# Linear attention with memories and experts on one core: values in tiles of their own, spare rows stored early, and local sums issued together with the memories

## The chip, the cores and the metric

The kernel runs on one core of a Trainium2 chip. The metric is the device time of one execution in microseconds (us). A core has five engines that run side by side: TensorE (PE in the profile; its weight loads are PEld), VectorE (DVE), ScalarE (ACT), GpSimd (POOL) and SyncE (SP), which issues most DMAs. Each engine works through its own instructions in the order of the program.

## The reference

All arithmetic is float32. The input is x with 4 batches of 1024 tokens and 256 channels; the attention has 16 heads of 16 channels and 4 memories, the expert part 8 experts of 176 hidden channels, two for each token, and a shared expert of 352.

```python
xn = layernorm(x)
q, k, v = split(xn @ w_q.T), split(xn @ w_k.T), split(xn @ w_v.T)
sq, sk = elu(q) + 1, elu(k) + 1
# memories: a coarse one (the sum of the four) and a weighted mean of the four
coarse = (sq @ M) / clip(sq . z);  M, z = memories.sum(0), norms.sum(0)
fine = sum_m w[m] * (sq @ memories[m]) / clip(sq . norms[m]);  w = softmax(mean over tokens)
p = sigmoid(relu(coarse @ eg_w1.T + b1) @ eg_w2.T + b2)
memory_output = p * fine + (1 - p) * coarse
# causal linear attention in chunks of 128, carrying the state S and its norm z
scores = (sq_c @ sk_c.T) * tril
local = (scores @ v_c + sq_c @ S) / clip(scores.sum(-1) + sq_c . z)
S, z = S + sk_c.T @ v_c, z + sk_c.sum(0)
attn = (gate * memory_output + (1 - gate) * local) @ w_o.T
# experts
cw = top-2 of softmax(xn @ gate_weight.T), normalised
y = sum_e cw[e] * down_e(silu(gate_e(xn)) * up_e(xn)) + shared expert of xn
out = x + attn + y
```

## The kernel before

**Tiles.** The 4096 tokens are 8 blocks of 512 (`blk`), each of 4 tiles of 128 (32 tiles, `n`). The heads' sums of values carry a column of ones, so a head has 17 columns in a `va` tile.

**Order.** The whole program is written out in order by Python code. Small functions each issue one unit of work. A unit is a tuple of a weight, a function and its arguments. `mix` merges several streams of units: each unit gets the rank (weight done before it + half its own) / (weight of its stream), and the streams are merged by rank. Nothing reorders the instructions afterwards. A tile pool with `bufs=k` for a tag has k buffers; a new tile of the tag waits until an old one is free of its last reader.

**The part ahead.** A string of words, `ahead`, lists the order in which blocks are prepared: `S4a` and `S4b` are `statistics` of the halves of block 4 (the mean and variance of two tiles each on VectorE; after the second, `rstd` is made by a VectorE add at L330 and a GpSimd power at L331), `N4` is `normalize` (a `shift` on VectorE at L338, two tiles normalized by VectorE at L345 and two by ScalarE at L350, the DMA of the block into `xns` in DRAM at L354, and two of the waiting loads of `loads`), `T4` is `transpose_x`, which transposes on TensorE and copies by ScalarE to `xnT`, and `V4a`, `V4b` are `values`, which multiply two tiles each by `wvg` on TensorE (L384). ScalarE copies the result to `va` (L389) and the router's logits to `lgs` (L393), and GpSimd writes ones and zeros (L394, L395). `va` lies in the same tile as the block's x (`wide`, tag `tok` of the pool `big`, 8 buffers): the values overwrite the normalized rows. Other words of the string are `masks`, `memories`, `living`, `route`, `exps` and `gates`.

**After it.** SP issues eight DMAs that copy x into `sums` in DRAM (L1250), then two that store zeros to the spare rows of `sums` and of `xns` (L1251, L1252). The zeros lie in the tile `zero`, of the tag `wide` with 3 buffers, which `count_i`, the exponentials of `project` (L627, L628) and `shared_gate` use as well. Then a first merge runs the first projections (`project` on TensorE, `projected` on VectorE) beside the steps of `sorting`, which rank the tokens by expert. `batch_weights` and `odd_keys` end it.

**Rounds.** `attention_round(n)` is the list of units of tile n: `scores` (TensorE, into the PSUM tile `quad`, of which there is one; it also needs the odd heads' keys `skO` from ScalarE, L700), four `mask` (VectorE reads `quad`, L720), `turned(n - 2)`, `keys_back`, `output(n - 2)` for n - 2 below `held_from` = 24, `memory` (TensorE, over `quad`, L828), `weigh` (VectorE, L838 to L843), `gate_hidden(n - 1)` (L903 to L909), `fine` in two halves (VectorE reads `quad`, L857), `local` (TensorE, L739, and a ScalarE copy, L746), `gate_out(n - 1)` (L915 to L918), `back` (L755 to L779), `update` and `odd_keys(n + 1)`. In rounds 0 and 1 the units of `lists` are merged in: for each batch of three tiles, `invert` makes one-hots on VectorE (L562, L566), `hold` scales them on ScalarE and GpSimd (L579, L582), and `add_slots` adds them up in the PSUM tile `found` (L590). In rounds 2 to 29 the experts are merged in: `expert_turn` (L1061 to L1067), `expert_hidden` (L1074 to L1081), `expert_out` (L1087, L1091) and `put`, a scatter that adds into `sums` (L1096). `level`, `cap` and `share` decide how much of the experts' work each round gets, by the weights of its units. Rounds 30 and 31 and what is left of the outputs follow, with additions of the expert sums on GpSimd (`total`) and the stores. Small PSUM results share a pool of 4 banks (`bank`).

Of the kernel before, what the change touches and what calls it, by code (L numbers as in the profile page):

```python
# [22 lines left out]
def linear_attention_moe_kernel(  # L23
# [62 lines left out]
    big = ctx.enter_context(tc.tile_pool(name="big", bufs=NBLK))  # L86
# [13 lines left out]
    def load_x(blk):  # L100

        wide = big.tile([P, NT, VW], FP, tag="tok", name=f"x_{blk}")
        xb = wide[:, :, :H]
        parts = 2 if blk == 0 else 1
        n = NT // parts
        for part in range(parts):
            rows = slice((blk * NT + part * n) * P, (blk * NT + (part + 1) * n) * P)
            (nc.scalar if part else nc.sync).dma_start(
                xb[:, part * n : (part + 1) * n],
                x[rows, :].rearrange("(n p) h -> p n h", p=P),  # L110
            )
        st["x", blk] = xb
        st["wide", blk] = wide
# [25 lines left out]
    wk = load_weight(w_k, "wk")  # L139
    b2 = const.tile([P, 1], FP, tag="b2", name="b2")  # L140
# [174 lines left out]
    def statistics(blk, half):  # L315

        xb = st["x", blk]
        if half == 0:
            st["norm", blk] = (
                small.tile([P, NT, 2], FP, tag="mv", name=f"mv_{blk}", bufs=3),  # L320
                small.tile([P, NT], FP, tag="rstd", name=f"rstd_{blk}", bufs=3),
            )
        mv, rstd = st["norm", blk]
        n = NT // 2
        for i in range(half * n, (half + 1) * n):
            stats = small.tile([P, 6], FP, tag="stats", name=f"stats_{blk}_{i}")
            nc.vector.bn_stats(stats, xb[:, i, :])
            nc.vector.bn_aggr(mv[:, i, :], stats)
        if half:
            nc.vector.tensor_scalar(rstd, mv[:, :, 1], LN_EPS, None, ALU.add)  # L330
            nc.gpsimd.tensor_tensor(rstd, rstd, neghalf, ALU.pow)  # L331

    def normalize(blk):

        xb = st["x", blk]
        mv, rstd = st.pop(("norm", blk))
        shift = small.tile([P, NT], FP, tag="shift", name=f"shift_{blk}")
        nc.vector.scalar_tensor_tensor(  # L338
            shift, mv[:, :, 0], -1.0, rstd, ALU.mult, ALU.mult
        )  # L340
        xnT = io.tile([P, NC, TB], FP, tag="xnT", name=f"xnT_{blk}")
        st["xnT", blk] = xnT
        half = NT // 2
        for i in range(half, NT):
            nc.vector.tensor_scalar(  # L345
                xb[:, i, :], xb[:, i, :], mv[:, i, 0:1], rstd[:, i : i + 1],
                ALU.subtract, ALU.mult,
            )
        for i in range(half):
            nc.scalar.activation(  # L350
                xb[:, i, :], xb[:, i, :], AF.Identity,
                bias=shift[:, i : i + 1], scale=rstd[:, i : i + 1],
            )
        nc.sync.dma_start(  # L354
            xns[blk * TB : (blk + 1) * TB, :].rearrange("(n p) h -> p n h", p=P), xb
        )
        for _ in range(2):
            if loads:
                loads.pop(0)()
# [14 lines left out]
    def values(blk, pair):  # L374

        xnT, wide = st["xnT", blk], st["wide", blk]
        if pair == 0:
            st["va", blk] = wide[:, :, : NH * D1].rearrange("p i (h k) -> p i h k", k=D1)
        va = st["va", blk]
# [14 lines left out]
        nc.gpsimd.memset(va[:, tiles, :, HD:D1], 1.0)  # L394
        nc.gpsimd.memset(wide[:, tiles, NH * D1 :], 0.0)  # L395
# [154 lines left out]
    def invert(lo):  # L550
# [3 lines left out]
        if lo == 0:  # L554
            st["found"] = bank("found")
# [31 lines left out]
    def add_slots(lo):  # L587
        places, held = st.pop(("held", lo))
        for k in range(min(3, 2 * NTT - lo)):
# [231 lines left out]
    def memory(n):  # L821
# [3 lines left out]
        for c in range(NC):  # L825
            for g in range(NG):
# [4 lines left out]
                )  # L831

# [343 lines left out]
    def attention_round(n):  # L1176
# [10 lines left out]
        u += unit(1280, output, n - 2, False) if n - 2 < held_from else []  # L1187
        u += unit(560, memory, n) + unit(64, weigh, n)

        u += unit(256, gate_hidden, n - 1) + unit(64, fine, n, 0)  # L1190
        u += unit(560, local, n) + unit(64, fine, n, 1)
# [30 lines left out]
    ahead = "S0a S0b S1a N0 T0 S1b S2a N1 V0a T1 V0b S2b S3a N2 V1a T2 V1b masks S3b S4a N3 V2a T3 V2b"  # L1222
    ahead += " memories S4b S5a N4 V3a T4 V3b living S5b S6a N5 V4a T5 V4b route exps S6b S7a N6 V5a T6"
    ahead += " V5b S7b N7 V6a T7 V6b gates V7a V7b"
# [4 lines left out]
    with tc.tile_pool(name="ps_v", bufs=2, space=bass.MemoryType.PSUM) as ps_v:  # L1229
        for what in ahead.split():  # L1230
# [3 lines left out]
            blk, half = int(what[1]), "ab".find(what[2:])  # L1234
            if what[0] == "S":
                statistics(blk, half)
            elif what[0] == "N":
                normalize(blk)
            elif what[0] == "T":
                for pair in range(NT // 2):  # L1240
# [10 lines left out]
    nc.sync.dma_start(sums[T:, :], zero[:, :H])  # L1251
    nc.sync.dma_start(xns[T:, :], zero[:, :H])  # L1252


    def sorting():
# [4 lines left out]
        yield from owners()  # L1260

    first_pairs = queries(0) + queries(1) + keys(0) + shared(0) + keys(1) + queries(2)
# [15 lines left out]
    batches = list(range(0, 2 * NTT, 3))  # L1278
    for k, lo in enumerate(batches):
        lists += [(400, invert, lo)]  # L1280
        lists += [(100, hold, batches[k - 1])] if k else []
        lists += [(768, add_slots, batches[k - 2])] if k > 1 else []
# [10 lines left out]
    def weight(units):  # L1293
        return sum(u[0] for u in units)
# [86 lines left out]
```

## Time and profile before

| | us |
|---|---|
| median of 3 runs | 717.58 |
| lowest and highest run | 713.74, 719.43 |
| the profiled execution's own time | 711.61 |
| its span, first to last instruction | 709.9 |
| TensorE busy | 653.3 |
| VectorE busy | 451.6 |
| GpSimd busy | 387.9 |
| ScalarE busy | 267.0 |

The mean granted clock of TensorE is 0.979. The part ahead ends about 54 us into the span, the first projections and the sort about 93, rounds 0 and 1 about 146, and round 29 about 660. A wait is put down to the instruction whose end released the waiting one.

### The profile page before, as it was taken

Reading aid. Unit: us, or ns where it says so; the run is one execution under the profiler, and the core shown is the slowest. Engines: PE = TensorE matmul, PEld = TensorE weight load, DVE = VectorE, ACT = ScalarE, POOL = GpSimd, SP = SyncE. Lnnn points to the kernel's source line nnn. Section 1 sums busy time; section 2 is a strip of 40 time slices with the busy share of each in tenths; the row PEclk is TensorE's granted clock in tenths of the full one; section 3 lists DMA queues with packets and bytes.
Section 4 is the critical chain, followed back from the end, with each engine's and each line's share of the span. In section 5 each row is a group of like instructions: output and inputs, shape, how many; then the busy total and the mean of one; then the engine's idle time right before and its main releaser. Section 6 shows DMA issues by size and latency. Waiting matters only on the chain.

```text
span 709.9 us, 14253 instructions
## 1 busy us (share of the span) xinstructions
PE 653.3 (92%) x5084; PEld 465.9 (66%) x5084; DVE 451.6 (64%) x1196; ACT 267.0 (38%) x614; POOL 387.9 (55%) x439
## 2 busy tenths in 40 slices
PE   4897979989999989999999999999898998898986
PEld 3773456667777766676676666677676775566665
DVE  5654878856666667665756756655767665556653
ACT  2663354424444344334333343344334433323310
POOL 3310036446776745565655645657767576556556
PEclk9999999999999999999999999999999999999999
DMA  9556000045556643343453443455555474553474
GB/s 301 181 184 193 0 1 1 24 125 141 133 137 135 137 90 92 85 100 90 92 110 81 103 92 80 98 123 126 105 136 117 112 169 88 129 118 65 96 236 166
DMA packets 86483, 81.52 MB, mean 115 GB/s; under 512 B 7549, under 2 KB 84013, under 8 KB 86285
## 3 DMA queue, kind: packets, MB, share of 16 engines
q1 hardware_dynamic: 71085, 60.40, 29.3%
q0 software_dynamic: 13632, 18.62, 15.8%
q10 hardware_dynamic: 1696, 1.58, 0.7%
q8 instruction: 41, 0.67, 0.4%
q14 instruction: 29, 0.24, 0.1%
HBM read 62.62 MB, written 22.15 MB: 119 GB/s over the span
## 4 chain that ended last, share of the span: by engine, by line
PE 78%; DVE 10%; DMA 4%; ACT 4%; issue 2%; POOL 1%; SPq 1%; DVEq 0%; ACTq 0%; POOLq 0%
PE phe L1074 12%; PE pye L1087 9%; PE po L980 6%; PE psu L943 6%; PE pg L929 5%; PE quad L713 5%; PE pk L622 4%; PE pn L739 4%; PE po L984 4%; PE quad L828 4%; PE pq L622 3%; PE pte L1061 2%; PE found L590 2%; PE pv L384 2%; PE pte L1065 2%
## 5 line engine op out<-in xcount | busy, mean ns | idle before, releaser
L1096 POOL DMA_INDIRECT sums<-y,islot x71 | 113.4, 1597 | 71.2 <-DMA sums<-y,islot 33.7
L1074 PE MATMUL phe<-wgu,turned 128*128 128x352 f32 x276 | 97.6, 476 | 3.7 <-issue 2.3
L1080 DVE SCALAR_TENSOR_TENSOR hidden<-hidden,phe 128x176 f32<-128x176 f32 x71 | 23.8, 335 | 109.3 <-ACT hidden L1079 109.2
L720 DVE TENSOR_TENSOR sT<-quad,causal 128x512 f32<-128x512 f32 x128 | 80.5, 681 | 4.3 <-PE quad L713 3.9
L1028 POOL DMA_INDIRECT xg<-xns,islot x71 | 71.0, 1000 | 18.3 <-issue 9.8
L1087 PE MATMUL pye<-wdn,turned 88*128 88x256 f32 x284 | 76.4, 391 | 2.5 <-issue 2.4
L850 POOL TENSOR_TENSOR cg<-coarse,gates 128x256 f32<-128x256 f32 x32 | 24.5, 766 | 94.7 <-DVE h L907 59.8
L1074 PEld LDWEIGHTS phe<-wgu,turned 128*128 128x128 f32 x276 | 48.5, 192 | 26.8 <-issue 8.2
L1087 PEld LDWEIGHTS pye<-wdn,turned 88*128 88x128 f32 x284 | 49.6, 189 | 17.0 <-issue 10.9
L1091 ACT ACTIVATE y<-pye,wslot 128x256 f32<-128x256 f32 x71 | 33.6, 473 | 70.4 <-PE pye L1087 70.3
L868 POOL TENSOR_TENSOR fm<-fm 128x512 f32<-128x512 f32 x32 | 43.0, 1343 | 26.4 <-DVE fm L857 14.9
L1067 ACT COPY turned<-pte 128x512 f32<-128x512 f32 (+1 forms) x71 | 41.1, 578 | 35.1 <-PE pte L1065 33.1
L1079 ACT ACTIVATE hidden<-phe 128x176 f32<-128x176 f32 x71 | 22.6, 318 | 79.4 <-PE phe L1074 77.2
L980 PE MATMUL po<-wd,h 128*128 128x256 f32 (+1 forms) x192 | 48.3, 388 | 0.1
L929 PE MATMUL pg<-xnT,wg 128*128 128x512 f32 (+1 forms) x96 | 47.7, 621 | 0.1
L943 PE MATMUL psu<-xnT,wu 128*128 128x512 f32 (+1 forms) x96 | 46.2, 603 | 0.0
L582 POOL TENSOR_TENSOR held<-ones,two 128x213 f32<-128x213 f32 (+1 forms) x22 | 15.6, 716 | 53.1 <-DVE ones L562 53.1
L857 DVE TENSOR_TENSOR fm<-quad,rw 128x512 f32<-128x512 f32 x64 | 42.0, 679 | 0.0
L980 PEld LDWEIGHTS po<-wd,h 128*128 128x128 f32 (+1 forms) x192 | 35.6, 194 | 6.9 <-issue 0.6
L828 PE MATMUL quad<-mem,sqT 32*128 32x170 f32 x512 | 28.2, 335 | 10.3 <-DVE sT L720 10.3
L838 DVE TENSOR_SCALAR rw<-quad 128x80 f32<-128x80 f32 x32 | 7.6, 238 | 45.0 <-PE quad L828 45.0
L918 DVE SCALAR_TENSOR_TENSOR o<-diff,prob,loc 128x256 f32<-128x256 f32 x32 | 33.3, 1042 | 3.6
(210 smaller groups left out, 1403.3 us busy)
## 6 DMA issues: line engine op xcount, KB each, us to landing
wgu<-in_w_gate_dram SPq DMA_DIRECT2D x71, 176.0 KB
wgu<-in_w_up_dram SPq DMA_DIRECT2D x71, 176.0 KB
wdn<-in_w_down_dram SPq DMA_DIRECT2D x71, 176.0 KB
xns<-x SPq DMA_DIRECT2D x8, 512.0 KB
sums<-in_x_dram SPq DMA_DIRECT2D x8, 512.0 KB
x<-in_x_dram SPq DMA_DIRECT2D x7, 512.0 KB
part<-sums SPq DMA_DIRECT2D x12, 256.0 KB
out_dram<-acc SPq DMA_DIRECT2D x12, 256.0 KB
```

The source lines that it names most:

```text
L622: nc.tensor.matmul(pq, w[:, k, c * P : (c + 1) * P], xnT[:, k, :], start=(k == 0), stop=(k == NC - 1),)
L720: nc.vector.tensor_mul(sT, quad[:, g, :].rearrange("p (c t) -> p c t", t=P), causal[:, None, :].to_broadcast([P, NC * 2, P]),)
L828: nc.tensor.matmul(quad[:, g, c * KM : (c + 1) * KM], sqT[rows, c, tok], mem[rows, c, :], start=True, stop=True,)
L857: nc.vector.tensor_mul(fm[:, c].rearrange("p g m (r k) -> p g (m r) k", k=HD), quad[:, :, c * KM + KX + KN : (c + 1) * KM].rearrange("p g ...
L868: nc.gpsimd.tensor_add(fm[:, :, 0:2, :], fm[:, :, 0:2, :], fm[:, :, 2:4, :])
L929: nc.tensor.matmul(pg[:n, :], wg[:, k, f * P : f * P + n], xnT[:, k, :], start=(k == 0), stop=(k == NC - 1),)
L943: nc.tensor.matmul(pu[:n, :], wu[:, k, f * P : f * P + n], xnT[:, k, :], start=(k == 0), stop=(k == NC - 1),)
L980: nc.tensor.matmul(po[:, :H], st["h", blk, f][:k, tok], wd[:k, f, :], start=(f == 0), stop=False)
L1028: nc.gpsimd.indirect_dma_start(out=xg, out_offset=None, in_=xns, in_offset=bass.IndirectOffsetOnAxis(ap=islot[:, j : j + 1], axis=0),)
L1074: nc.tensor.matmul(ph[:, : 2 * F], xgT[:, k, :], wgu[:, k].rearrange("p g f -> p (g f)"), start=(k == 0), stop=(k == NC - 1),)
L1087: nc.tensor.matmul(py[:, :H], hT[:FH, f, :], wdn[:, f, :], start=(f == 0), stop=(f == 1))
L1096: nc.gpsimd.indirect_dma_start(out=sums, out_offset=bass.IndirectOffsetOnAxis(ap=islot[:, j : j + 1], axis=0), in_=st.pop(("y", j)), in_of ...
```

## The change

It has four parts.

1. `big` has 9 buffers. `values` takes a tile of its own for each block (`va_b`) and no longer writes over x; GpSimd fills the ones and zeros of a whole block at once, at its first half.
2. The two stores of zeros move from behind the copies of x into the list `loads`, behind `wk`. `normalize` takes two of the loads for even and three for odd blocks.
3. The string `ahead` has another order: `N` stands in front of the next block's first half of statistics, and block 0 is taken in halves all the way. `normalize` gives tiles to ScalarE and VectorE by turns. The first two batches of the lists (`invert` of two and `hold` of one) move from rounds 0 and 1 to the last steps of `sorting`; the PSUM bank of `found` is taken at the first `add_slots`.
4. `memory` and `local` become one unit of weight 1120. Where a round has no `output` left, an empty unit of 1280 takes its place in the merge. `weight`, which feeds `level` and `cap`, does not count empty units.

```diff
-    big = ctx.enter_context(tc.tile_pool(name="big", bufs=NBLK))
+    big = ctx.enter_context(tc.tile_pool(name="big", bufs=NBLK + 1))
...
-        wide = big.tile([P, NT, VW], FP, tag="tok", name=f"x_{blk}")
-        xb = wide[:, :, :H]
+        xb = big.tile([P, NT, VW], FP, tag="tok", name=f"x_{blk}")[:, :, :H]
...
     wk = load_weight(w_k, "wk")
+    loads.append(lambda: nc.sync.dma_start(sums[T:, :], zero[:, :H]))
+    loads.append(lambda: nc.sync.dma_start(xns[T:, :], zero[:, :H]))
...
-        if half:
-            nc.vector.tensor_scalar(rstd, mv[:, :, 1], LN_EPS, None, ALU.add)
-            nc.gpsimd.tensor_tensor(rstd, rstd, neghalf, ALU.pow)
+        if half or blk == 0:
+            some = slice(half * n, (half + 1) * n) if blk == 0 else slice(0, NT)
+            nc.vector.tensor_scalar(rstd[:, some], mv[:, some, 1], LN_EPS, None, ALU.add)
+            nc.gpsimd.tensor_tensor(rstd[:, some], rstd[:, some], neghalf[:, some], ALU.pow)
...
-        for i in range(half, NT):
-            nc.vector.tensor_scalar(
...
-        for i in range(half):
-            nc.scalar.activation(
...
+        for i in range(some.start, some.stop):
+            if i % 2:
+                nc.vector.tensor_scalar(
...
+            else:
+                nc.scalar.activation(
...
+        if half == 0:
+            return
...
-        for _ in range(2):
+        for _ in range(2 + blk % 2):
...
         if pair == 0:
+            wide = big.tile([P, NT, VW], FP, tag="tok", name=f"va_{blk}")
+            st["wide", blk] = wide
+            nc.gpsimd.memset(wide[:, :, NH * D1 :], 0.0)
             st["va", blk] = wide[:, :, : NH * D1].rearrange("p i (h k) -> p i h k", k=D1)
+            nc.gpsimd.memset(st["va", blk][:, :, :, HD:D1], 1.0)
...
-        nc.gpsimd.memset(va[:, tiles, :, HD:D1], 1.0)
-        nc.gpsimd.memset(wide[:, tiles, NH * D1 :], 0.0)
...
+    def memory_and_local(n):
+
+        memory(n)
+        local(n)
...
-        u += unit(1280, output, n - 2, False) if n - 2 < held_from else []
-        u += unit(560, memory, n) + unit(64, weigh, n)
+        u += unit(1280, output, n - 2, False) if n - 2 < held_from else [(1280, lambda: None)]
+        u += unit(1120, memory_and_local, n) + unit(64, weigh, n)
...
-        u += unit(560, local, n) + unit(64, fine, n, 1)
+        u += unit(64, fine, n, 1)
...
-    ahead = "S0a S0b S1a N0 T0 S1b S2a N1 V0a T1 V0b S2b S3a N2 V1a T2 V1b masks S3b S4a N3 V2a T3 V2b"
-    ahead += " memories S4b S5a N4 V3a T4 V3b living S5b S6a N5 V4a T5 V4b route exps S6b S7a N6 V5a T6"
-    ahead += " V5b S7b N7 V6a T7 V6b gates V7a V7b"
+    ahead = "S0a S0b N0a T0a N0b T0b S1a S1b N1 S2a V0a T1 V0b S2b N2 S3a V1a T2 V1b masks S3b N3 S4a"
+    ahead += " V2a T3 V2b memories S4b N4 S5a V3a T4 V3b living S5b N5 S6a V4a T5 V4b route exps S6b N6"
+    ahead += " S7a V5a T6 V5b S7b N7 V6a T7 V6b gates V7a V7b"
...
-    nc.sync.dma_start(sums[T:, :], zero[:, :H])
-    nc.sync.dma_start(xns[T:, :], zero[:, :H])
...
         yield from owners()
+        invert(batches[0])
+        yield
+        hold(batches[0])
+        invert(batches[1])
+        yield
...
-    for k, lo in enumerate(batches):
-        lists += [(400, invert, lo)]
-        lists += [(100, hold, batches[k - 1])] if k else []
-        lists += [(768, add_slots, batches[k - 2])] if k > 1 else []
+    for k, lo in enumerate(batches[2:]):
+        lists += [(400, invert, lo), (100, hold, batches[k + 1]), (768, add_slots, batches[k])]
...
     def weight(units):
-        return sum(u[0] for u in units)
+        return sum(u[0] for u in units if len(u) > 2)
```

## The prediction

> **What bounds the kernel.** First the page's busy rows and the chain by engine: TensorE sets the time, but not all of it.
>
> ```profile
> PE 653.3 (92%) x5084; PEld 465.9 (66%) x5084; DVE 451.6 (64%) x1196; ACT 267.0 (38%) x614; POOL 387.9 (55%) x439
> PE 78%; DVE 10%; DMA 4%; ACT 4%; issue 2%; POOL 1%; SPq 1%; DVEq 0%; ACTq 0%; POOLq 0%
> ```
>
> The edits leave TensorE's instructions as they are, so a gain can only come from its 57 us of idle time (709.9 - 653.3) and from stretches at a lower granted clock. I looked for both with the waits of two windows (columns: total us, times, longest us), the chain, and the busy time by stretch. The waits of 0 to 110 us:
>
> ```profile
> DVE sqT L636 <- ACT eq L628: 9.2, 3, 7.2
> ACT eq L627 <- DMA xns<-zero: 7.0, 1, 7.0
> PE pk L622 <- DVE sqT L636: 3.9, 1, 3.9
> PE found L590 <- ACT held L579: 3.6, 1, 3.6
> ```
>
> ScalarE's third exponential needs a buffer of tag `wide` that `zero` still holds; VectorE waits for that exponential, TensorE for VectorE. The chain shows why `zero` is held: its last store is queued behind eight copies of x into `sums`.
>
> ```profile
> 48.96 6.13 DMA sums<-in_x_dram
> 55.11 10.66 DMA xns<-zero
> 65.84 0.61 ACT eq L627
> ```
>
> The stretches (start:end, length, busy of PE, PEld, DVE, ACT, POOL, clock, DMA share, GB/s) show what such a gap costs afterwards:
>
> ```profile
> 65.00:70.00 5.00, 2.11 (x4) 0.86 (x5) 2.68 (x9) 3.46 (x6) 0.00 (x0) 0.86 0.02 8
> 70.00:75.00 5.00, 5.00 (x11) 2.27 (x10) 4.79 (x14) 1.82 (x3) 0.00 (x0) 0.80 0.02 5
> 95.00:100.00 5.00, 5.00 (x45) 3.94 (x45) 4.03 (x9) 2.34 (x9) 2.74 (x4) 0.66 0.01 3
> 605.00:610.00 5.00, 3.61 (x22) 2.19 (x23) 1.68 (x5) 0.65 (x2) 2.59 (x2) 0.79 0.69 161
> ```
>
> At 0.66 of full clock 1.7 us of the five are lost (0.34 x 5). A dense slow spell therefore costs about 1.7 us beyond its gap.
>
> In the middle TensorE is nearly full (98.48 us busy of 100 from 350 on). Only late rounds stand out; from 575 to 655, first the waits of PE, then the timeline of round 26 (start, duration, instruction, in brackets the idle time before it and what ended it):
>
> ```profile
> PE quad L828 <- DVE sT L720: 7.9, 4, 2.4
> 586.08 0.34 DVE L1080 SCALAR_TENSOR_TENSOR hidden<-hidden,phe 128x176 f32<-128x176 f32 x1 [2.82 <-ACT hidden L1079]
> 586.70 1.28 DVE L720 TENSOR_TENSOR sT<-quad,causal 128x512 f32<-128x512 f32 x2
> 588.04 0.86 PE L828 MATMUL quad<-mem,sqT 32*128 32x170 f32 x16 [2.04 <-DVE sT L720]
> ```
>
> `memory` overwrites `quad`, so it waits for all four masks, and the last two masks stand in VectorE's order behind an expert's `hidden`, which waits for TensorE and ScalarE. Rounds 26 to 29 have no `output` between the masks and `memory`.
>
> **The change, part by part.**
>
> *Values apart (`va_b`, a ninth `tok` buffer) and the new order ahead.* Today `va_0` overwrites x_0 and waits for the store of x_0 (4.8 us on ScalarE at 17.57; GpSimd's `rstd` of block 2 queues behind it). `va_0` takes the free buffer, and `va_b` needs only the store of x_(b-1): that wait goes. But normalize now stands ahead of the next block's first statistics:
>
> ```profile
> 34.00 0.17 DVE L330 TENSOR_SCALAR rstd<-mv 128x4 f32<-128x4 f32 x1
> 34.08 0.42 DVE L327 BATCH_NORM_STATS2 stats<-x 128x6 f32<-128x256 f32 x1
> 34.32 1.01 POOL L331 TENSOR_TENSOR rstd<-rstd,neghalf 128x4 f32<-128x4 f32 x1 [5.20 <-DVE rstd L330]
> 35.36 0.16 DVE L338 SCALAR_TENSOR_TENSOR shift<-mv,rstd 128x4 f32<-128x4 f32 x1
> ```
>
> The 1.36 us from 34.00 to 35.36 are covered by two statistics (1.16) today and will be bare. A block then costs VectorE 2.3 (statistics) + 1.36 + 0.85 (shift, two tiles) = 4.5 us, where TensorE needs 4.4 (transposes 0.87, values 3.56); masks, memories, route and gates add 7.7 us of VectorE. Walking the order: N1 ends at 13.1, N4 at 28.7, N5 at 35.3, N7 at 47.3-47.9; then T7 and three halves of values, 0.9 + 5.4, give 53.7. Today V7b ends at 54.16. The bare wait eats what the freed buffer gives. I take 0, from -1.5 to +1.5. Halving block 0 and alternating the two engines by tile only move the first transposes about 1 us ahead.
>
> *Spare rows stored early.* The two 128 KB stores now enter SP's queue behind N1 and N2 (issue 0.51 and 0.34 us, ahead of later weight loads needed only after 53 us and of later xns stores with a slack of some us). `zero` is free long before 59 us. The third exponential then starts near 59.3 instead of 65.84. TensorE saves its 3.9 us of idle and the slow spell, 1.7: -5.6. Next is VectorE, whose first late result moves by 6.3 us (67.14 to 60.8), so it does not hold TensorE. If the buffer stayed late, all 5.6 would return. Take -5.6 (bounds -6.5, -3.5). The copies into `sums` go on from 48 to 66; the first scatter into them comes after 150.
>
> *First two lists ahead of time.* Today `found` waits behind the chain of `batch_weights` on VectorE (90.7 to 93.2), then a one-hot (0.92) and ScalarE's 0.84. With two one-hots and one `hold` in the sort's steps, TensorE can run `add_slots(0)` and the next gate projection at once and next misses only the odd keys (ScalarE, behind the exponential of 91.49): scores at 92.2. What is done today by 97.08 is done at 93.3: -3.8, and about 1 us of the spell at 95-99: -4.5 (taken a little short). The added VectorE work in the sort is 2 x 0.92 us; from 85 to 90 VectorE is busy only 2.43 of 5, so it fits; uncovered it costs 1.8. Bounds -6, -2.
>
> *`local` behind `memory`, and the empty unit of 1280.* No instruction is added. The empty unit counts in the ranks of the merge, not in a round's weight; the other empty unit (3000 of the experts) stops counting too, which lowers the level from 11824 to 11724 and leaves the number of experts in every round as it is. From the weights in the listing the ranks follow: in rounds 26 to 29 no `hidden` stands between the masks any more, and between the last mask and `memory` stand 4.4, 4.4, 2.7 and 4.4 us of TensorE work (an expert product 1.2, a shared projection 1.72, `expert_out` 0.86, a turn 0.65), where nothing stood. That covers the four waits, 7.9 us. What is late next is `quad`'s return: `memory` to the next scores shrinks from about 10 to 7 us of TensorE work, and VectorE's chain (weigh 2.3, h 0.5, fine 1.3, an interposed `hidden`) takes 5.2 to 7.4. I keep 1 us for that.
>
> In rounds 2 to 25 masks already end 2.4 to 7.4 us before `memory`. In some, `hidden` now stands ahead of `weigh` (9, 11, 12, 13, 22 to 25): VectorE starts about 2.6 us later there, against a measured slack of 2.1 to 4.9 before the next scores. Conversely rounds 2, 8 and 21 lose a 2.4 us wait of `weigh`. Taken +0.6 (bounds -3, +4); uncovered, each us late is paid by TensorE.
>
> *The rule that speaks against part of this.* Two of the gaps (605 and 630) are followed by slow spells, together 3.4 us. The Trainium skill, page "TensorE: Matmul & The Clock Gate", section "Why this matters for your kernels", puts the fall at idle gaps of over about 3 us. By it, closing gaps of 1.7 us returns no clock, and this edit gives 7.9 - 1 = 6.9. The row 605:610 shows 0.79 right after a single gap of 1.74 us; by it the edit gives 7.9 + 3.4 - 1 = 10.3. Measurement decides; as a new gap may bring one such spell back, I take -9.5 (bounds -12, -4).
>
> *The tail.* Round 31's `memory` waits 2.47 us for masks at 683.02, and its spell costs 1.7; `output` 25 now covers the wait. But the ranks also put `turned(30)` ahead of output 27, and `gate_hidden(31)` with `turned(31)` behind 29 and ahead of 30. The first meets o(30) about 1.8 us early; the second bares h 0.76, prob 0.29 + 0.14, o 0.62 and the hand-overs, 2.2 us. -4.2 + 4.0: 0 (bounds -2.5, +2.5).
>
> **Sum:** 0 - 5.6 - 4.5 - 9.5 + 0.6 + 0 = -19.0. The profiled execution took 711.61 (span 709.9 and 1.7 around it), so it would take 692.6. The runs' median is 717.58, 6 us above that execution; the same -19 gives **698.6**.
>
> **Rivals.**
>
> *Only the beginning gains (0.17).* The late rounds hand `quad` back late instead, and gaps of 1.7 us return at the scores. For it: one buffer, and `memory` now 3 to 4 us later. Against: covers of 6.4 to 8.4 us. Then 0 - 5.6 - 4.5 + 0 = -10: 707.5.
>
> *More than forecast (0.12).* The other two spells of the rounds (skO 2.31 us at 544, the wait of `pye` 2.40 at 504) also vanish, as back and turn shift: -19 - 8 = 690.6. Nothing in the edits aims at them.
>
> *The stores do not free the buffer (0.05).* Another reader of that slot keeps it: -19 + 5.6, 704.2. Against: the wait names `zero`'s store alone.
>
> *Slower: `weigh` behind `hidden` (0.06).* Were it late in all 28 rounds, VectorE's 2.6 us against slacks of 1.0 to 1.4 us (rounds 4, 6, 8 and 14) would bare 1.2 us a round: 34 us, and six more spells, 10. 698.6 + 44 = 743. It decides once the mean loss passes 19 / 28 = 0.68 us a round. Against: only about eight rounds have that order, most with slack above 2.6.
>
> **Numbers.** The forecast has 0.60, its own range 692 to 705 (parts' bounds seldom all on one side). The wider range takes in the rivals at 690.6, 704 and 707.5 and a run's scatter of about 3 us (713.74 to 719.43 now): 689 to 711. About 1%, 7 us, is what this kernel's measurement can tell from no change. Faster by more: 0.58 of the forecast's 0.60, 0.14 + 0.12 + 0.04 of the rivals: 0.88; within: 0.06; slower: 0.06.
>
> **What would show it.** Right: no wait of ScalarE for `zero`, no slow stretch near 70 and 97; the first gather of xg near 136 instead of 146; no wait of L828 for sT from 565 to 640; the values ending within 1.5 us of 54; two new gaps of about 2 us ahead of L882 in the tail. Wrong: waits of L713 for `fm` at round boundaries, slow stretches in the middle beyond the two at 505 and 546, VectorE waiting in `rstd` until the values end past 56.

## The result, and the profile after

The changed kernel takes **711.65 us** (median of 20 runs, 710.04 to 716.87) against 717.14 for the kernel before on the same chip: a ratio of 0.9936, with a 95% interval of 0.9915 to 0.9958. That is 5.5 us less, where 19 had been forecast. The profiled execution of after has a span of 709.3 us and stands near its median. The one of before (711.61, span 709.9) was 5.5 us quicker than its median, so the two traces show a difference of 0.6 us where the medians show 5.5. Every set of runs below has its own runs of the kernel before (medians of 712.5 to 717.1), so ratios are compared across sets, not times.

The page of after, its busy row and the chain by engine:

```profile
PE 648.7 (91%) x5084; PEld 466.2 (66%) x5084; DVE 453.2 (64%) x1198; ACT 267.0 (38%) x614; POOL 386.4 (54%) x424
PE 69%; DVE 20%; issue 4%; ACT 3%; POOL 2%; DMA 1%; DVEq 0%; POOLq 0%; ACTq 0%
```

TensorE is busy for nearly as long as before (4.6 us less). But the chain that ended last now runs through VectorE for 20% of the span, where it was 10%.

The places that the prediction aimed at did change. The waits of 0 to 110 us in after (columns: total us, times, longest us), the rows on which the first part turns:

```profile
DVE sqT L646 <- ACT eq L638: 3.3, 4, 1.9
DVE shift L346 <- POOL rstd L334: 8.8, 8, 1.2
```

and of before, for the second of them:

```profile
DVE shift L338 <- POOL rstd L331: 5.4, 2, 4.3
```

No engine waits for the store of `zero` any more: VectorE's wait for the exponential is 3.3 us in place of 9.2, and the wait of `pk` for it is gone. The wait for `rstd` is now bare at every block, eight times for 8.8 us, where before had two for 5.4. The stretches of after that answer to the slow ones of before (start:end, length, busy of PE, PEld, DVE, ACT, POOL, clock, DMA share, GB/s):

```profile
65.00:70.00 5.00, 5.00 (x13) 2.10 (x12) 4.69 (x16) 3.05 (x5) 0.00 (x0) 1.00 0.02 5
70.00:75.00 5.00, 5.00 (x13) 2.17 (x12) 4.83 (x14) 1.01 (x2) 0.00 (x0) 1.00 0.00 0
95.00:100.00 5.00, 4.70 (x63) 3.38 (x63) 4.46 (x10) 2.71 (x9) 2.56 (x4) 1.00 0.01 3
605.00:610.00 5.00, 4.12 (x52) 3.31 (x50) 3.75 (x8) 1.46 (x3) 4.69 (x6) 1.00 0.33 87
```

The gap at 65 and the slow clocks of 0.80, 0.66 and 0.79 are gone; in the clock records of after no slow spell (a stretch at half clock) begins between 552.8 and 709.8. Round 26 in after's timeline: the last masks, the `hidden` that stood ahead of them, `memory`:

```profile
591.42 1.88 DVE L730 TENSOR_TENSOR sT<-quad,causal 128x512 f32<-128x512 f32 x3
595.77 0.34 DVE L1095 SCALAR_TENSOR_TENSOR hidden<-hidden,phe 128x176 f32<-128x176 f32 x1 [2.48 <-ACT hidden L1094]
598.33 0.86 PE L838 MATMUL quad<-mem,sqT 32*128 32x170 f32 x16
```

The masks end at 593.3, 5.0 us ahead of `memory`; that `hidden` now follows them. So what took the gain back lies elsewhere. Set the stretch from the scores of round 9 to those of round 26 ("scores 9 to 26" from here on) side by side, first before, then after:

```profile
267.00:580.00 313.00, 303.88 (x2526) 218.25 (x2525) 201.48 (x509) 117.96 (x257) 188.47 (x183) 0.99 0.46 106
```
```profile
263.00:589.00 326.00, 306.91 (x2522) 222.33 (x2522) 199.92 (x508) 117.29 (x257) 184.59 (x181) 0.97 0.45 101
```

The same work (2522 and 2526 recorded matmuls) takes 13 us longer. TensorE's idle time, length less busy, grows from 9.1 to 19.1 us, its busy time by 3.0, and the clock falls from 0.99 to 0.97. In the clock records, two slow spells became five. The sum over the whole span, in us, between the same events in both traces:

| from, to | before | after | difference | forecast |
|---|---|---|---|---|
| start, end of `values` | 54.16 | 55.60 | +1.4 | 0 |
| end of `values`, first `pr` (stores early) | 34.4 | 29.0 | -5.4 | -5.6 |
| `pr`, scores of round 0 (lists ahead) | 6.8 | 3.0 | -3.8 | -4.5 |
| scores 0, scores 3 | 66.3 | 69.2 | +2.9 | in the +0.6 |
| scores 3, scores 26 | 418.7 | 432.2 | **+13.5** | +0.6 |
| scores 26, scores 30 | 81.5 | 74.2 | -7.3 | -9.5 |
| scores 30, last `po` | 42.5 | 42.9 | +0.4 | 0 |
| last `po`, end | 5.5 | 3.2 | -2.3 | not named |

Together -0.6, between these two executions: one row has eaten what the others brought.

### The profile page after: what moved, and what is told of

It is laid out like the page before. It is cut to its first block, busy times and chain, and to the rows that moved or that the text cites. A ratio compares the mean times of both kernels' runs of the same rounds, so it can differ in the third digit from the quotient of the medians.

```text
span 709.3 us, 14219 instructions
## 1 busy us (share of the span) xinstructions
PE 648.7 (91%) x5084; PEld 466.2 (66%) x5084; DVE 453.2 (64%) x1198; ACT 267.0 (38%) x614; POOL 386.4 (54%) x424
## 4 chain that ended last, share of the span: by engine, by line
PE 69%; DVE 20%; issue 4%; ACT 3%; POOL 2%; DMA 1%; DVEq 0%; POOLq 0%; ACTq 0%
PE phe L1089 11%; PE pye L1102 8%; PE po L995 5%; PE pn L749 4%; PE psu L958 4%; PE quad L723 4%; PE pg L944 4%; PE quad L838 4%; PE po L999 4%; PE pk L632 3%; PE pq L632 3%; PE pte L1076 3%; DVE o L933 3%; PE pt L897 2%; DVE fm L872 2%
## 5 line engine op out<-in xcount | busy, mean ns | idle before, releaser
L1043 POOL DMA_INDIRECT xg<-xns,islot x71 | 70.8, 997 | 19.1 <-issue 10.3
L1089 PEld LDWEIGHTS phe<-wgu,turned 128*128 128x128 f32 x276 | 49.8, 197 | 27.8 <-issue 8.6
L933 DVE SCALAR_TENSOR_TENSOR o<-diff,prob,loc 128x256 f32<-128x256 f32 x32 | 45.3, 1416 | 3.9 <-issue 0.5
L1094 ACT ACTIVATE hidden<-phe 128x176 f32<-128x176 f32 x71 | 22.5, 317 | 63.1 <-PE phe L1089 53.4
L944 PE MATMUL pg<-xnT,wg 128*128 128x512 f32 (+1 forms) x96 | 45.4, 596 | 0.1
L756 ACT COPY nT<-pn 128x512 f32<-128x512 f32 x32 | 18.7, 585 | 47.6 <-PE pn L749 41.8
L749 PE MATMUL pn<-sT,va 128*32 128x128 f32 x1024 | 34.8, 276 | 0.0
```

The lines of the kernel that those rows point to most:

```text
L749: nc.tensor.matmul(pn[CW * r : CW * (r + 1), q, :], wide[:, i, first : first + CW], st["sT", h // 2][:, c * 2 + h % 2, :], start=True, sto ...
L933: nc.vector.scalar_tensor_tensor(o, st.pop(("diff", n)), prob, st.pop(("base", n)), ALU.mult, ALU.add)
L944: nc.tensor.matmul(pg[:n, :], wg[:, k, f * P : f * P + n], xnT[:, k, :], start=(k == 0), stop=(k == NC - 1),)
L1043: nc.gpsimd.indirect_dma_start(out=xg, out_offset=None, in_=xns, in_offset=bass.IndirectOffsetOnAxis(ap=islot[:, j : j + 1], axis=0),)
L1089: nc.tensor.matmul(ph[:, : 2 * F], xgT[:, k, :], wgu[:, k].rearrange("p g f -> p (g f)"), start=(k == 0), stop=(k == NC - 1),)
```

## The experiments

The question is which part of the change holds back rounds 3 to 25: the merged unit, the empty unit, or the order ahead; and once that is known, by what mechanism. In the diffs the lines with a minus are after's, in one case before's.

### One part undone at a time

`local` back in its own unit between the two halves of `fine`, the empty units kept:

```
-u += unit(1120, memory_and_local, n) + unit(64, weigh, n)
+u += unit(560, memory, n) + unit(64, weigh, n)
...
-u += unit(64, fine, n, 1)
+u += unit(560, local, n) + unit(64, fine, n, 1)
```

> The changed kernel with memory and local as two units again, weigh behind memory and local between the halves of fine; the empty units of 1280 stay. Theory A (the merged unit sends weigh behind an expert's hidden on VectorE and brings back's bank back late, which costs TensorE about 13 us from round 12 to 27): about 700 us, 10 to 13 below the changed kernel, weigh again within 0.3 us of memory's end in rounds 9, 11, 12, 13 and 22 to 25. Rival B (the loss of the middle is scatter between executions and local's place does not matter): 710 to 713.

Measured: 698.23 us, ratio 0.9743 (0.9706 to 0.978). The stretch from scores 9 to scores 26 is 312.5 us again, and the late rounds keep their gain (scores 26 to 30 in 73.4). So the loss came with the merged unit; whether by ranks, by VectorE's queue or by the place of `local` is asked below.

The empty unit of 1280 taken out instead:

```
-u += unit(1280, output, n - 2, False) if n - 2 < held_from else [(1280, lambda: None)]
+u += unit(1280, output, n - 2, False) if n - 2 < held_from else []
```

> The changed kernel without the empty unit of 1280 (rounds 26 to 31 then have nothing in the place of output). Theory A (the empty unit is what removed the four waits of memory for the masks, and it is worth 7 to 10 us): about 719, with waits of memory for sT of about 8 us from round 26 to 29. Rival B (the merged unit moves memory far enough by itself, and the empty unit adds only the two gaps in the tail): 709 to 712.

Measured: 712.17 us, 0.9939 (0.9916 to 0.9961), the same as after. The waits of TensorE from 575 to 655 still have nearly nothing of the masks:

```profile
PE quad L838 <- DVE sT L730: 0.9, 1, 0.9
```

So with the merged unit the empty one has little left to do: without it, scores 26 to 30 take 76.5 us in place of 74.2, and what follows 1.2 us less. A unit is ranked at the middle of its weight, so `memory` in a unit of 1120 is merged 280 later anyway, behind more of the experts' work, and `weigh` 560 later. That was the rival's reading.

The order ahead as in before (only the string `ahead`, cut here to its first part):

```
-ahead = "S0a S0b N0a T0a N0b T0b S1a S1b N1 S2a V0a T1 V0b S2b N2 S3a V1a T2 V1b masks ...
+ahead = "S0a S0b S1a N0 T0 S1b S2a N1 V0a T1 V0b S2b S3a N2 V1a T2 V1b masks ...
```

> The changed kernel with the old order of the part ahead (statistics of the next block ahead of normalize, block 0 whole); values keep their own tiles. Theory A (the bare wait for rstd cost 1.4 us or more, and it ate what the freed buffer gives): 2 to 4 us less than the changed kernel, the values ending near 52. Rival B (the part ahead is set by TensorE and by the slow spell near 37, not by VectorE's order): within 1 us of the changed kernel, the values ending at 55 to 56.

Measured: 708.49 us, 0.9896 (0.9855 to 0.9936); `values` end at 51.58 in place of 55.60. The interval overlaps that of after (0.9915 to 0.9958).

Before (the lines with a minus are before's), with nothing changed but the two stores and the number of loads that a block takes:

```
+loads.append(lambda: nc.sync.dma_start(sums[T:, :], zero[:, :H]))
+loads.append(lambda: nc.sync.dma_start(xns[T:, :], zero[:, :H]))
...
-for _ in range(2):
+for _ in range(2 + blk % 2):
...
-nc.sync.dma_start(sums[T:, :], zero[:, :H])
-nc.sync.dma_start(xns[T:, :], zero[:, :H])
```

> The kernel before with one edit: the two stores of zeros in the list of loads behind wk, and two or three loads a block. Theory A (the stall at 59 to 68 is worth 5.6 us and nothing downstream takes it back): 711.5, a ratio of 0.992. Rival B (VectorE, saturated until 85, or a later wait takes most of it): 714 to 717, a ratio over 0.995.

Measured: 712.25 us, 0.993 (0.9899 to 0.9961). From the end of `values` to the first `pr` its trace takes 28.5 us (54.10 to 82.63) against 34.4: -5.9, the size forecast.

The first and third of these together:

```
-u += unit(1120, memory_and_local, n) + unit(64, weigh, n)
+u += unit(560, memory, n) + unit(64, weigh, n)
...
-u += unit(64, fine, n, 1)
+u += unit(560, local, n) + unit(64, fine, n, 1)
...
-ahead = "S0a S0b N0a T0a N0b T0b S1a S1b N1 ...
+ahead = "S0a S0b S1a N0 T0 S1b S2a N1 ...
```

> The changed kernel with the old order ahead and with memory and local as two units again (values apart, stores, lists and empty units stay). If the two losses add: 698.2 - 3.2 = 695. If they overlap[...]: 697 to 699.

Measured: 688.18 us, **0.9632** (0.9595 to 0.9669). The sum expected, 695 where before took 716.5, is a ratio of 0.970; this is about 5 us better.

### Where the merged unit costs: ranks, VectorE's queue, or the place of `local`

Three edits of after. In the first, `memory` has 560 again, `weigh` follows it, and `local` follows `weigh`, all ahead of `fine`:

```
-u += unit(1120, memory_and_local, n) + unit(64, weigh, n)
+u += unit(560, memory, n) + unit(64, weigh, n) + unit(560, local, n)
```

> The changed kernel with the merged unit split: memory 560, weigh 64, local 560 directly behind, then gate_hidden and both halves of fine. Memory and weigh have their ranks of before; local still stands ahead of gate_hidden and of fine. Theory A (the rank of memory and weigh: weigh comes behind an expert's hidden): about 699, as with local back. Rival B (the place of local: TensorE does it early and then reaches back and the next bank before VectorE has caught up): 708 to 712.

Measured: 704.28 us (697.01 to 712.27, widely spread), 0.9834 (0.979 to 0.9879): between, as neither theory had it. `weigh` is in time here: in its trace it starts 0.07 us after `memory` in rounds 9, 11 to 13 and 22 to 25. But `gate_hidden` and the first `fine` now rank 560 later, and that seems to cost here too. It is not the whole answer: a kernel further below (`weigh` inside the merged unit) has these two equally late and is quick; it differs from this one only in the places of `memory` and `local`. What holds this kernel back stays open.

In the second, `local` stays behind `memory` but both count 560, and an empty counted unit of 560 stands where `local` was, so that every rank is the old one:

```
-u += unit(1120, memory_and_local, n) + unit(64, weigh, n)
+u += unit(560, memory_and_local, n) + unit(64, weigh, n)
...
-u += unit(64, fine, n, 1)
+u += unit(560, lambda m: None, n) + unit(64, fine, n, 1)
```

> The changed kernel with the merged unit at weight 560 and an empty unit of 560 (counted in the level) where local was, between the halves of fine. All other units have the ranks that they have with local back; only local is issued with memory. Theory A (ranks): 698 to 700. Rival B (the place of local in TensorE's order): 708 to 712. Between: both.

Measured: 693.51 us, 0.971 (0.9668 to 0.9751), as good as `local` put back, within the intervals. Where TensorE does `local` does not show in the time; the ranks of the others do.

In the third, `gate_out` is put ahead of the second half of `fine`, which keeps VectorE's `o` away from GpSimd's half of `fm`:

```
-u += unit(64, fine, n, 1)
-u += unit(64, gate_out, n - 1) + unit(528, back, n) + unit(300, update, n)
+u += unit(64, gate_out, n - 1) + unit(64, fine, n, 1)
+u += unit(528, back, n) + unit(300, update, n)
```

> The changed kernel with gate_out ahead of the second half of fine, so that o no longer runs beside GpSimd's sums of fm. Theory C (o, 1416 ns a time instead of 1042 with GpSimd beside it, lengthens the chain to back's loc and so the hold on the bank, about 0.4 to 1 us in many rounds): o falls to about 0.5 us and the time by 4 to 8 us, to 704 to 708. Rival A (the chain is late because weigh starts late; o's length is a small part): within 2 us of 711.7.

Measured: 709.83 us, 0.9925 (0.9884 to 0.9966): no gain over after that stands clear of the scatter. The groups of instructions, after and then this kernel (count | busy us, mean ns | idle before):

```profile
L933 DVE SCALAR_TENSOR_TENSOR o<-diff,prob,loc 128x256 f32<-128x256 f32 x32 | 45.3, 1416 | 3.9 <-issue 0.5
```
```profile
L933 DVE SCALAR_TENSOR_TENSOR o<-diff,prob,loc 128x256 f32<-128x256 f32 x32 | 16.4, 514 | 3.6
```

`o` fell from 1416 to 514 ns, 29 us of VectorE in all, and the median hardly moved. A slow `o` is not what cost the 13 us. It may be worth a part: at a mean clock of 0.983 to 0.985 this kernel took 703.4 to 703.8 us, where after at 0.983 took 710.2 to 712.4, and scores 9 to 26 take 319.5 us in its trace in place of 326.2, with `weigh` as late as in after. About 2 us of that may be the set of runs: at 0.979, before took 711.0 to 712.3 in this one and 713.4 to 714.8 in the one with `local` back. At 0.966 to 0.974 the kernel took 711.1 to 714.2, so slow spells decide more about its median than `o` does.

### `weigh` itself

If the late rank of `weigh` is the cause, a kernel with `memory` at its old rank and `weigh` 560 later must be slow, and one that brings only `weigh` forward must be quick. In the first of the two, `gate_hidden` and the first `fine` stand behind `weigh` and are 560 later with it; the second is the cleaner test.

```
-u += unit(1120, memory_and_local, n) + unit(64, weigh, n)
+u += unit(560, memory_and_local, n) + unit(560, lambda m: None, n) + unit(64, weigh, n)
```

> The changed kernel with memory and local merged at weight 560 and then an empty unit of 560 (counted in the level), so that memory and local stand where they did with the merged unit of 560, and weigh and fine are as late as in the changed kernel. Theory A1 (the late rank of weigh on VectorE is the cause): ratio 0.988 to 0.996, like the changed kernel. Theory A2 (the late rank of memory on TensorE): 0.968 to 0.975, as with the merged unit at 560.

Measured: 722.79 us, 1.0089 (1.0059 to 1.0119): slower than before, and far from the quick kernels. It is worse than the range that I had put down. From scores 9 to 26 it takes 327.3 us, as after does (326.2); the rest is lost earlier, where scores 0 to 9 take 184.3 us against 175.3. Rounds 0, 2, 3 and 8 account for it (9.3 us; the others win 0.3 back). In rounds 2 and 8 `weigh` starts 4.45 and 3.40 us after `memory` here, and 0.40 and 0.22 in after.

The opposite, `weigh` put into the merged unit, with its weight added (so that `memory` itself ranks 32 later), and the order ahead of after:

```
+def memory_local_weigh(n):
+    memory_and_local(n)
+    weigh(n)
...
-u += unit(1120, memory_and_local, n) + unit(64, weigh, n)
+u += unit(1184, memory_local_weigh, n)
```

> The changed kernel with weigh inside the merged unit: memory and local are as late as in the changed kernel, but weigh stands directly behind them on VectorE, ahead of an expert's hidden of the same stretch. Theory A1 (weigh behind hidden): ratio 0.970 to 0.978. Theory A2 (memory's late rank): 0.988 to 0.996. With both, between the two.

Measured: 691.29 us, **0.9626** (0.9575 to 0.9677), better than the range expected. Against before, this is a larger gain than the one forecast for the change, and it is after with one unit changed. Scores 9 to 26, 310.4 us:

```profile
260.00:570.00 310.00, 298.52 (x2522) 216.92 (x2522) 196.25 (x506) 117.17 (x257) 186.63 (x183) 0.99 0.46 107
```

TensorE is idle for 11.5 us in place of 19.1 and busy 8.4 us less, at a clock of 0.99. There is one slow spell where after has five; at the prediction's 1.7 us each, the four make about 6.8 of the 8.4 (an estimate). How many spells a run has varies: the mean clock of this kernel's runs lies between 0.978 and 0.995.

What VectorE waits for in that stretch tells the mechanism. First before, then after, then this kernel:

```profile
DVE hidden L1080 <- ACT hidden L1079: 51.3, 23, 5.4
DVE rw L838 <- PE quad L828: 38.5, 11, 4.9
```
```profile
DVE hidden L1095 <- ACT hidden L1094: 80.8, 23, 7.7
DVE rw L853 <- PE quad L838: 4.2, 2, 2.7
```
```profile
DVE rw L858 <- PE quad L838: 40.6, 12, 4.9
DVE hidden L1100 <- ACT hidden L1099: 38.0, 21, 4.9
```

`rw` is the first instruction of `weigh`. In before, VectorE comes to it early and waits there for `memory`, 38.5 us in all. In after it hardly waits there: it stands at an expert's `hidden`, with `weigh` queued behind, while `quad` is long ready. Without that, the 40 us of waiting are back at `rw`, where VectorE waits for TensorE and not TensorE for VectorE. The late-`weigh` kernel shows after's picture (83.6 at `hidden`, 4.2 at `rw`), the one with all ranks of 560 shows before's (53.5 and 37.5).

Round 22 shows a single case. After's timeline (start, duration, instruction, idle time before it and its releaser), with `memory`, the expert's `hidden`, `weigh`, `o`, `loc` and TensorE's next `pye`:

```profile
517.96 0.86 PE L838 MATMUL quad<-mem,sqT 32*128 32x170 f32 x16
521.60 0.34 DVE L1095 SCALAR_TENSOR_TENSOR hidden<-hidden,phe 128x176 f32<-128x176 f32 x1 [7.05 <-ACT hidden L1094]
522.22 0.23 DVE L853 TENSOR_SCALAR rw<-quad 128x80 f32<-128x80 f32 x1
526.35 1.89 DVE L933 SCALAR_TENSOR_TENSOR o<-diff,prob,loc 128x256 f32<-128x256 f32 x1
528.89 0.42 DVE L783 TENSOR_TENSOR loc<-pb,rden 128x256 f32<-128x256 f32 x1
529.37 1.13 PE L1102 MATMUL pye<-wdn,turned 88*128 88x256 f32 x4 [0.99 <-DVE loc L783]
```

The same round with `weigh` in the unit:

```profile
507.92 0.86 PE L838 MATMUL quad<-mem,sqT 32*128 32x170 f32 x16
509.15 0.24 DVE L858 TENSOR_SCALAR rw<-quad 128x80 f32<-128x80 f32 x1 [4.64 <-PE quad L838]
511.56 0.34 DVE L1100 SCALAR_TENSOR_TENSOR hidden<-hidden,phe 128x176 f32<-128x176 f32 x1 [0.61 <-ACT hidden L1099]
516.15 0.42 DVE L783 TENSOR_TENSOR loc<-pb,rden 128x256 f32<-128x256 f32 x1
517.11 1.13 PE L1107 MATMUL pye<-wdn,turned 88*128 88x256 f32 x4
```

`memory` ends at 518.82 in after, yet `rw` starts at 522.22, 3.40 us later, behind a `hidden` for which VectorE had waited 7.05 us. The lateness runs down VectorE's queue: `loc` ends 11.35 us after `memory`'s start in after and 8.65 here. TensorE's `pye`, which in after waits 0.99 us for it, comes without a wait. The waits of TensorE from 263 to 589 in after, those of over 1 us:

```profile
PE pye L1102 <- issue: 7.0, 4, 2.0
PE quad L723 <- ACT skO L710: 1.9, 2, 1.7
PE pte L1076 <- ACT y L1106: 1.9, 2, 1.3
PE pye L1102 <- DVE loc L783: 1.6, 2, 1.0
PE pu L818 <- ACT y L1106: 1.6, 2, 0.9
PE phe L1089 <- ACT turned L1082: 1.4, 3, 0.9
PE pte L1076 <- DVE h L922: 1.3, 2, 0.7
```

With the four smaller rows (`pr` on y 0.9, `pk` on `loc` 0.4, `pu` on h 0.2, `pye` on `quad` 0.7), the rows on h, `loc` and y add up to 7.9 us. With `weigh` in the unit none of them is there, and TensorE's idle time is 7.6 us less. The 7.0 us of `pye` with no releaser stay in that kernel:

```profile
PE pye L1107 <- issue: 5.9, 3, 2.0
```

So they are mostly not what the cure removes. The timeline tells what they wait for, here once in after:

```profile
485.66 0.42 DVE L783 TENSOR_TENSOR loc<-pb,rden 128x256 f32<-128x256 f32 x1
486.19 1.10 PE L1102 MATMUL pye<-wdn,turned 88*128 88x256 f32 x4 [1.54 <-issue]
```

`pye` starts 0.1 us after the end of `loc`. It is so each time: in the 16 traces there are 60 waits of `pye` of over 0.3 us that the profile puts down to no releaser or to a matmul, and all 60 end 0.10 us after a `loc`. So they are waits for `loc` as well, and they go with the place of `local`. The five kernels that issue `local` between the halves of `fine` have one of them, of 2.4 us; the eleven that issue it earlier have five each. Yet that does not show in the time (all ranks of 560: 0.971; `local` back: 0.9743). That `pye` waits for `loc` because the bank which back's `pb` holds until `loc` has read it is needed again is my reading of these rows; no run isolates it.

### What the parts are worth in the best versions

`local` back and the old order ahead, without the empty units; against the kernel of 0.9632:

```
-u += unit(1280, output, n - 2, False) if n - 2 < held_from else [(1280, lambda: None)]
+u += unit(1280, output, n - 2, False) if n - 2 < held_from else []
```

> The kernel with the old order ahead and local back (ratio 0.963), without the empty unit of 1280. Theory A (with memory at its old rank the empty unit removes the four waits for the masks, and with the merged unit those waits were removed by the merged unit's own later rank): 7 to 11 us more, a ratio of 0.973 to 0.979. Rival B (the empty unit is worth nothing in either case): a ratio of 0.961 to 0.966.

Measured: 705.01 us, 0.982 (0.978 to 0.986), a little more than the range expected. The waits of 575 to 655:

```profile
PE quad L838 <- DVE sT L730: 7.9, 4, 2.4
```

This is the row of before to the tenth of a microsecond. So once `memory` has its own 560 back, the empty unit is worth 0.982 / 0.9632 = 1.0195, about 13 us. In the two traces scores 26 to 30 differ by 8.9 us (80.0 and 71.1). Another 4.2 us lie in scores 9 to 26, where both kernels issue the same work and this one has two more spells' worth of slow clock: that part is probably scatter.

All ranks of 560, and the old order ahead:

```
-u += unit(1120, memory_and_local, n) + unit(64, weigh, n)
+u += unit(560, memory_and_local, n) + unit(64, weigh, n)
...
-u += unit(64, fine, n, 1)
+u += unit(560, lambda m: None, n) + unit(64, fine, n, 1)
...
-ahead = "S0a S0b N0a T0a N0b T0b S1a S1b N1 ...
+ahead = "S0a S0b S1a N0 T0 S1b S2a N1 ...
```

> The merged unit at weight 560 with the empty unit of 560 where local was, and the old order ahead. If local's place is of no account and the old order is worth 3 us or more: a ratio of 0.962 to 0.967, the same as with local back and the old order (0.963).

Measured: 691.83 us, 0.964 (0.9597 to 0.9683).

`weigh` in the unit, and the old order ahead:

```
-u += unit(1120, memory_and_local, n) + unit(64, weigh, n)
+u += unit(1184, memory_local_weigh, n)
...
-ahead = "S0a S0b N0a T0a N0b T0b S1a S1b N1 ...
+ahead = "S0a S0b S1a N0 T0 S1b S2a N1 ...
```

> Weigh inside the merged unit and the old order ahead. If the two gains add (0.9936 to 0.9626 for weigh, 0.9936 to 0.9896 for the order): a ratio of 0.957 to 0.960. If they overlap: 0.961 to 0.966.

Measured: 689.76 us, 0.9646 (0.9586 to 0.9705): nothing beyond `weigh` in the unit alone.

The order ahead of after, with the statistics of the next block put in front of each normalize again from block 1 on; block 0 keeps its halves:

```
-... S1a S1b N1 S2a V0a T1 V0b S2b N2 S3a V1a T2 V1b masks S3b N3 S4a ...
+... S1a S1b S2a N1 V0a T1 V0b S2b S3a N2 V1a T2 V1b masks S3b S4a N3 ...
```

> The changed kernel with one move in the order ahead: from block 1 on the first half of the next block's statistics stands ahead of normalize again; block 0 stays in halves, the tiles stay alternated. Theory A (the bare wait for rstd is what the new order costs): the values end near 52 to 53.5, a ratio of 0.988 to 0.991. Rival B (the halves of block 0 or the slow spell near 37 cost it): the values end at 55 to 56.5, a ratio of 0.992 to 0.996.

Measured: 708.5 us, 0.9935 (0.9903 to 0.9967): in the total the same as after, which misses theory A's ratio. But the values end at 51.44, as with the old string (51.58). So the bare wait for `rstd` is what moves them, and the halves of block 0 cost them nothing. Both kernels were profiled without a slow spell near 43 us. The kernel without the empty unit, also without that spell, ends its values at 53.73 in the new order: 2.1 to 2.3 us for the bare wait. Of the executions that have the spell, those in the new order end at 55.4 to 56.6 and those in the old at 53.6 to 54.2.

## Why the prediction was wrong in size, point by point

**Rounds 2 to 25 are the step that failed.** It named the right rounds (9, 11, 12, 13, 22 to 25) and the right cause, `weigh` behind `hidden`. It sized the lateness at 2.6 us; measured from `memory`'s end, it is 3.40, 4.00, 3.40 and 3.40 in the first four and 3.40 in the last four. (Rounds 2, 8 and 21 did lose their wait of 2.4 us, as forecast.) The term went wrong in the next half sentence: "against a measured slack of 2.1 to 4.9 before the next scores". That slack does hold: the next scores never waited for `fine`, and in the tightest round 0.20 us was left. But `weigh` is not used by the scores alone. h, `o`, `rden` and `loc` stand behind it on the same engine, and for these TensorE waits within the same round. I had measured one consumer of VectorE's queue and charged nothing for the others. +0.6 was taken, with +4 as the bound; from scores 3 to 26 it was +13.5. Of the 13 us from scores 9 to 26, 10.0 are idle time of TensorE and 3.0 more busy time, with three more slow spells. That the lateness of `weigh` is the cause is shown by the kernel that moves it alone back (0.9626 against 0.9936); the waits of `pye` for `loc` (2.4 us in before, 9.3 in after, 7.1 in that kernel) mostly go with `local`'s new place, which the +0.6 left out too. The rival "`weigh` behind `hidden`" carried this mechanism too. It priced it by the scores as well, and so asked for all 28 rounds to be late; ten of them (9, 11 to 13, 22 to 25, 28 and 29) and rounds 0 and 1 were enough to take most of the gain, though not to turn the sign.

**The late rounds** gave -7.3 of -9.5. The reason given was incomplete: the ranks of the merged unit alone already move `memory` behind the masks (0.9 us of waiting left without the empty unit). Where `memory` keeps 560, the empty unit does it, as forecast. `weigh` was late by 3.40 us in rounds 28 and 29 too; with the cure, scores 26 to 30 take 71.5, 10.0 less than before.

On the clock, the weighing against the Trainium skill ("TensorE: Matmul & The Clock Gate", "Why this matters for your kernels") goes to the row: gaps well under the page's bound of about 3 us do bring slow spells here. After's gap of 1.54 us, which ends at 486.19, stands in front of one, which begins at 488.0:

```profile
485.00:490.00 5.00, 3.81 (x43) 3.23 (x44) 3.13 (x12) 0.66 (x2) 4.41 (x6) 0.80 0.30 87
490.00:495.00 5.00, 5.00 (x21) 4.02 (x20) 2.55 (x6) 1.78 (x4) 2.55 (x2) 0.86 0.58 146
```

So a new gap can cost twice, which the +0.6 left out: three of after's five spells in scores 9 to 26 (467.5, 488.0, 508.4) begin about 2 us after a wait of `pye` for `loc`.

**The stores** gave -5.4 of -5.6, and -5.9 alone. This step was right with its reason.

**The lists ahead** gave -3.8 of -4.5 up to the first scores. The first gather of `xg` was put near 136 and came at 142.74, mostly because round 1 lost 4.1 us to the merged unit: scores 0 to `islot` (the last result that the gather needs) take 50.5 us in before, 54.6 in after and 49.8 with `weigh` in the unit, where the gather comes at 137.97. The same step thus pays for this miss.

**The order ahead** was taken as 0 from -1.5 to +1.5 and came out at +1.4. Against the old string, the bare wait costs 2.1 to 2.3 us in the traces. In the total its worth stays open: the old string gains in after itself (0.9896 against 0.9936, overlapping), with all ranks of 560 (0.971 to 0.964, overlapping) and with `local` back (0.9743 to 0.9632), and nothing with `weigh` in the unit (0.9626 and 0.9646); removing the bare wait alone gains nothing either (0.9935).

**The tail** was a sum of two terms near 0, and +0.4 to the last `po` is that sum. The waits of 660 to 710:

```profile
PE pt L897 <- DVE o L933: 2.2, 1, 2.2
PE pt L897 <- DVE rden L779: 1.1, 1, 1.1
```

The two new gaps stand where they were put, 2.2 us as worked out and 1.1 for 1.8. The 2.3 us after the last `po` were not foreseen.

With `weigh` in the merged unit, all other steps being the same, the trace is 22.5 us shorter than before's (687.4 against 709.9) and the ratio is 0.9626. The largest term that the sum of -19 lacked is what else stands behind `weigh`.

## What to carry to other kernels

When a small unit is merged by its rank into a strictly ordered engine, look at what stands ahead of it: `weigh` needs 2.3 us of VectorE, and behind another chain's wait it cost about 22 us of 711 (0.9936 against 0.9626). Lateness on an engine must be charged to every consumer of everything queued behind, not to the one reader of the moved result. And when the weights of units set the order, joining two units also moves all that follows by the weight added ahead of it: keep short hand-overs inside the unit whose result they read, or leave the weight where it was. Here both worked (0.9626 and 0.971).

## What the hardware showed that I had not expected

In the clock records, TensorE's slow spells run at half clock. All within before and after last 3.413 us, but for those that the end of the program bounds; in eight of the 16 traces some last two or three times as long (6.83 and 10.24 us). Within one execution their starts lie whole multiples of 3.413 us apart (in after 467.5, 488.0 and 508.4: 20.48 = 6 x 3.413).

Whether a gap is followed by a spell is not a matter of its length alone. Gaps of 1.74 us (before, ahead of 607.9) and 1.54 us (after, ahead of 488.0) had one, while in before gaps of 2.04 us (ending at 588.04) and 2.35 us (at 649.74) had none. How a gap falls on that grid fits these four. The first two lie whole in one step of the grid, in which TensorE is then busy for only 0.49 and 0.55 of the time. The other two fall across two steps, with 0.59 and 0.82, and 0.57 and 0.74. Over all 16 traces, from 30 us on, each of the 46 steps at full clock with TensorE busy under 0.40 was followed by a spell, and none of the 2774 with 0.72 or more; of the 198 between, 58 were. The busy share therefore does not decide alone in that middle range. The same small shift of the work can thus gain or lose a spell, which probably makes part of the scatter between executions of one kernel; no run here tests that.

`o`, 256 elements a partition, takes 0.48 us with GpSimd idle or at a gather or scatter. Where it starts beside GpSimd's sum of `fm`, it ends about 0.3 us after that sum, most often after 1.45 us: that made the 1416 ns against 514 of its group.
